# Two heads per 32-row strip, mixing folded into weights, last experts added by matmul: an edit of a two-layer hybrid kernel

## The chip, the cores and the metric

The kernel runs on one core of a Trainium2 chip. Its time is the device time of one launch in microseconds (us). The kernel before takes 791.38 us (median of three runs, 787.01 to 791.51).

## The reference

Input x is 4×256 rows of 256 f32 values. Eight residual stages follow each other, each fed by a layer norm without weights:

```python
x = x + attn_a0(norm(x))   # A: token mixing of neighbours, then a recurrence
x = x + ffn0(norm(x))      # F: the best of 8 experts, 256x256
x = x + attn_b0(norm(x))   # S: state space, with a convolution of 4 taps
x = x + ffn0(norm(x))      # G
x = x + attn_a1(norm(x))   # a: causal attention, 16 heads of 16, 4 key groups
x = x + ffn1(norm(x))      # e: the best 4 of 32 experts, width 96
x = x + attn_b1(norm(x))   # b: as a, with a slope per head times the distance
x = x + ffn1(norm(x))      # f
```

In stage A the change touches this part (xs is x shifted by one row; sequences are 256 rows):

```python
k = (x*tmk + xs*(1-tmk)) @ Wk.T + bk      # v likewise; r through silu
t = max(u + k, w)
e1, e2 = exp(-w - t), exp(u + k - t)
a = e1*a + e2*v ; b = e1*b + e2           # a recurrence over the rows
```

In stage S it touches conv = sum over 4 taps of shifted rows times conv_w, plus a bias, then silu, for 512 channels of h and 64 each of B and C. In f, y of an expert is (silu(x·gate)·(x·up))·down and is added with the weight of that expert among the row's four.

## The kernel before, in words

The 1024 rows are two groups g of 512, two sequences each, as four tiles of 128 rows. The residual x[g] stays on chip. Every stage of every group is a set of Python generators ("streams") named by stage letter, group and part: a0p is attention a, group 0, part p. follow() (L119) draws one step of a stream after another by the hand-written list ORDER. All engines work in order, so this one list is the program order of PE (TensorE), DVE (VectorE), ACT (ScalarE), POOL (GpSimd) and SP (which issues DMAs). BANKS is a second list: it says, tile by tile, which of the eight 2 KB PSUM banks is used. Nothing is reordered after it.

norm_steps (L221) makes mean and variance on DVE, the inverse root on POOL, the four normalised tiles xn on DVE (L239), then transposes them on PE and copies them as xnT on ACT.

Stage A, shift_mix (L265): mix(j) makes the mixed inputs for k, v, r (j = 0, 1, 2), each in two halves c: ACT scales the shifted rows (L293), DVE adds the own rows (L295). keys (L302) projects, makes low = min(k+u-w, 0) and top = max(k+u, w) on DVE (L308, L311), their exponentials on ACT, two scans and a reciprocal on DVE. values (L328) projects and scans, receive (L346) multiplies with r.

Stage S, state_space: conv (L588) has six channel tiles, four of 128 channels and B and C of 64 each; per tile a projection, an ACT scaling, three shifted multiply-adds on DVE (L602) and a silu.

Attention (L774), per group and layer: keys project all four key groups into kT, 32 rows each (16 dimensions, then rows that carry the key's number and causal flags), and keep it four times in kb, each copy with one key group unmasked (two copies by ACT L804, two by DVE). queries makes four projections pq, one head of each key group at a time (c), scaled into qT. Then four query units of 128 rows (sequence b, query tile qt; w = 128 or 256 keys). peaks (L842): scores pS as matmuls on 64 rows (L851; two strips r of the array side by side, masks in kb keep the two key groups apart), then for each head a DVE maximum (L864), which the profile shows as a maximum `junk` and a small read `nmx`. below (L870) transposes the maxima into the queries, qm. weights (L883): scores again, transposed, pST (L893, two strips at a time), ACT exponentials pT (L901), POOL's causal cut on the diagonal (L904). products (L909): pctx, four column strips of the array. finish divides, transposes, projects with Wo.

second_ffn (L984), stages e and f: route makes the four experts of a row and its place (128 places per expert). send scatters the rows by 16 indirect DMAs of POOL into `sent` in DRAM (L1046). For each of 16 pairs of experts: SP fetches xe (L1073), PE transposes, gate and up pgu, ACT silu, DVE product, PE transpose ph, DVE copy hT, PE py (L1118), DVE copy ye, SP writes `done` (L1124). back gathers by 16 indirect DMAs of POOL (L1134), add multiplies and adds on DVE (L1144), leave writes out.

Two matters decide the order around the change. First, SP's queue: in e and f the first fetch of group 1, which needs all 16 of its scatters, stands ahead of group 0's last done writes. Second, `sent` must have been cleared (stream cl, 512 KB writes) and the weights loaded (la, lf, ls, l1, lw) by SP at places in the same list.

Of the kernel before, what the change touches and what calls it, by code (L numbers as in the profile page):

```python
# [30 lines left out]
ROWS = E1 * CAP  # L31
NH, HP, NS = 8, 64, 64
# [3 lines left out]
UNITS = ((0, 0), (0, 1), (1, 1), (1, 0))  # L36


ORDER = """
k1 A0n kf x0*2 kf A1n A0n*2 x0 A0n x0 A0n*3 la A0n*4 lf x1 A1n x1 A0n ka A0m0 x1 A1n*2 A0n*2 A0m0  # L40
x1 A1n*2 A0m0 la lf A0m0 A0k0 A0m2*2 A1n*3 A0m1 A1n A0m1*3 A1n*2 A1m0 A0k0*4 A0k1*5 A0k0*2 ls A0k0
la A0v0 A1m0 la lf*2 A1n lf A1n A1m0*2 A0m2 A0b A0v0*2 A0k1 kf A0v0*2 A0k1 A0m2 ls A0k1 A0m2 ls*2
A1k0*3 A0v1 A0r0*2 A0v1*2 A1k0 A0v1 lf A0v1 A0r1*2 A1m1 A1k1 la A0o A1k1*4 A0o*4 F0r*2 A0o*3 F0r*2
A1m1*2 F0r A1m1 A1v1 lf*2 F0r A1k1*2 A1m2 F0r*3 A1v0 A1v1*3 F0r*3 A1k1 A1v1 k1*2 ks kf*3 F0r*5 ls
k1 A1k0*2 A1m2*4 F0r*3 F0s*4 A1v0*2 F0f A1v0 A1k0*2 A1v0 A1r0*2 A1r1*2 A1b A1o*3 F1r A1o ks*3
A1o*3 F1r*2 F0f F0t A1o F1r*2 PS F0t*2 F0f*2 F0t*2 F1r*4 F0e F1r*3 lf F0e*2 F0t F0e*2 F1r*5 F0e*2
F0r F0t F1r*4 F1s F0e*2 F1s F0t F0e*3 F1s*2 F0w F0b F0a S0n F0b*2 F1f F0a F0b F0a S0n*2 F0a S0n
F1f S0n F1t*3 F1w F1e F1t F1f*2 F1t ks*2 S0n*8 F1e*3 F1t*3 S0d*2 F1e*3 S0d*5 S0u*2 S0c*3 S0h S0u
S0c*2 F1e*2 S0h*2 S0g*2 S0h F1e*2 S0h*5 S0c*5 F1e S0h*4 F1b S0g*5 F1a S1n F1b*3 S0g k1 F1a S0c*2
F1a S1n*2 F1a S1n*2 cl*2 S0h*4 S0d*2 S1n*3 k1 S0l*2 S1n S0m*4 k1 S0l*3 S0h*3 k1 S0h cl S0h*2 S1n*4  # L50
S0l cl S0l*3 S1g*2 S1c S1d*2 S1c*4 S0u*2 S0h S0v*2 S0l*2 S0v S1d S0v*3 S0l S0v S0l S1d S0u*2 S1d
S0o S0u S1h S0v*5 S0y S1h S0o*2 S0y*2 S0l*2 S0y S0z S0o S1c S1h S1g S0z*2 S1h S0z S1d S1h S1c
S1h*4 S0l S0z S1c S0o*3 S1h S0z*4 S1c*2 S0z S1h S0z*3 S0y S0z*4 l1*2 G0r S1d S0l*4 S1u*2 S0l S1c
S1h*6 S1c S0z*2 S0l G0r S0l S1u*2 S1h*3 cl S0l S0y*2 S1h*3 S0y S0z*2 S1h l1 S0z S0o S0z S1g*2 S1d
cl S1v S1d S1v*7 S1m*4 S1l*2 S0z*5 S1l*2 cl S0z*4 S1v*2 S0z*2 S1u*2 S0z*2 G0r S1v*2 S1l*3 S0z*2
G0r*2 S1l*5 S1o S1y*2 G0r S1u G0r S1u G0r*2 S1y*2 S1z G0r*4 k1 S1o*3 S1z*3 G0r S1g*3 G0r*4 S1z
G0r*2 G0w G0s*4 S1z G0f S1z*3 S1l G0f S1z*2 S1l*10 S1z*5 S1l S1z S1y*3 S1z*2 S1o*3 G0t S1y G0f
G0t*2 G0f l1 S1z*2 G0e*3 G0t*2 S1z G0t G0e*2 G0t*2 G0e S1o S1z*2 G0e*2 G1r*2 S1z G0e*4 S1z*10 l1
S1z*3 G0b G1r G0b G1r*2 G0b*2 G1r*6 G0a k1*3 G1r*3 G0a a0n*2 G0a a0n G0a a0n*9 G1r*3 a0n a0k a0q
G1r P2 a0q cl a0a cl*2 a0q*5 G1r*2 G1w a0k*5 a0p k1 G0r k1 a0p k1 G1s a0p cl*2 a0q a0p*7 a0v l1*2  # L60
a0b G1r a0b cl*3 a0p*2 a0v a0p G1s*3 G1f G1t*2 G1f G1t*2 a0p*3 G1f G1t G1f a0p*3 G1e*6 G1t*2 a0b
G1e*2 a0p G1e G1t G1e*2 a0p*4 a0w*6 a0b a0p*5 a0w*4 a0c a0p G1e G1b*3 G1a*2 a1n a0w G1b a0w*6
a0b*2 a0c a0f*3 G1a a1n*2 a0w*3 cl G1a lw*3 a0w*9 a0c a1n a0w a1n*2 a0w*3 a0p a0w*4 a0f a1n*4
a0p*2 a0f a1a a0p a0f*2 a1n*3 a0f e0r a0p*2 a0c a1k a0w*4 a0b a0f a0b a1k a0f a1q*4 a0w*4 a0c
a0w*4 a1q a1k a0f a1k*3 a0w*3 a1p*2 a0f*2 a1q a0f e0r a0f*3 l1*2 a1q*2 a0f*2 a1p*4 a0c a0f*5 a1p*2
a0f*3 a1p a0f e0r*3 a1b*2 a1p e0r*4 a1w*5 a1p*3 e0r a1p*2 e0r*9 a1w a1v*2 a1w*2 a1p*2 a1w e0r*3
a1w a1c a1f a1p*2 a1b*2 e0s a1p*5 e0s*4 a1p a1w*7 a1p*4 e0s*2 a1p*3 a1w*2 a1c lw*2 e0s*3 a1w*3 e0s
a1p*2 a1w*4 lw*4 a1b*2 a1w*3 a1f*2 a1w a1f*2 a1p*2 a1c a1w*3 a1c a1f lw e0s*3 e0w a1f*2 e0s*2 a1b
lw*2 e1r lw a1f*2 a1w*5 a1f a1b a1w*10 a1c a1f*5 e0f*2 e0t e0f*2 a1w*2 a1f a1w e0t a1w a1c a1f e0t
a1f*5 e0t a1f e0g a1f*2 e0g*4 a1f e0t*4 e0h e0g a1f e1r*4 e0h*3 e0g*4 e0f*2 e0t e1r*4 e0g e0d*2  # L70
e1r*4 e0d*2 e1r e0h e0d*2 e0g e0t e1r*2 e0g e0h*3 e0t*2 e1r*2 e0g e1r e0f*3 e0d*2 e0g*4 e0t*2 e0f
e0t e0d*2 e0t*2 e1r*2 e1s*5 e0h*3 e0g*4 e0t*2 e0f e0d*4 e1s e0g*2 e0f e0g e0t*3 e0f e1s e0f e0h*4
e0d*2 e0g e0d e1s*2 e0g*4 e0d*3 e0t*2 e0h e0g e0t*3 e0h*3 e0d*2 e0f*2 e0h e0g*3 e0d*3 e0g e1s*2
e0g e0d*5 e0h e0g e0h*2 e0t*4 e0g*2 e0d*2 e0g e0d e0h*3 e0d*2 e1s*4 e0d e1s e1f*2 e0g*4 e0h*2 e0d
e0g e0d e0t e0g*2 e1f e0h e0d*2 e0g e0h e0d e0h*2 e0d*3 e1t*3 e1f e0d*2 e1t e1g*2 e0d*2 e0b e1t*2
e1g*2 e1t e1h e1g*3 e1f e1h*2 e1f e1g e1h e1d*2 e1f e0b*2 e1d*2 e1g e1t e1g*3 e1t*2 e0b e1t*3
e1h*3 e1d e1g e1h e1f*3 e0a*4 b0n e1g*4 e1t e1d*2 e1t*2 e1d*3 e0b*2 e0a e1d*2 e0a e1h*2 e0b e0a
e1g*5 e1t*3 e1h e1g e1h e1f*3 e1g e0b*3 e1t e1d*5 e1h e1w e1h e0a b0n e1h e1g*3 e1t*2 e1d*2 e1h
e1g e1d e0b e1h e0b*2 e1t e1g e1d e1f e0a e1d e0b e1g*2 e0a*2 e1f e1t*2 e0b*2 e1d*2 e1h e1d e0a*5
e1t e1g*3 b0n*2 e1h*4 e1g*3 b0n e1g*2 b0n*4 e1d*2 e1t*2 e1d*2 b0a e1h*3 e1g e1t b0n*3 e1d*4 e1g*2  # L80
e1t e1d b0n b0q*2 e1g*3 e1d e1h*2 b0k*3 e1d*3 b0q*2 e1h b0k*2 b0q b0k b0p*2 b0q*3 e1f e1t b0p*3
e1t e1g*2 b0p e1g e1d e1h e1d e1h e1d b0b*2 e1h*2 b0p*3 b0w*4 e1d*5 b0p b0w*2 e1d b0p*4 b0w b0p*2
b0w b0p*2 b0w*2 b0v*2 b0b*2 e1d e1b e1a e1b*3 b0p*2 b0w b0p*4 e1a*2 e1b*2 b0w*2 b0c b0p*2 e1a e1b
e1a b0f*3 e1b e1a e1b b0p*4 e1b b0w*6 e1a b0c b0w*3 b0f b0p*3 b0w*4 e1a b0f*3 b0c b0f b0b*2 b0p*2
b0f*2 e1a*2 b0w*6 b0f*2 b0w*2 e1b*3 b1n b0c e1b*3 b0p b0b b0w*3 b0b e1a*3 b0w e1a b0w*6 e1a b0w*4
b0c e1a b0w*4 b1n*4 b0f*5 b1n*2 b0c b0f*3 b1n*3 b0f*4 b1n*3 b1k f0r b1k*3 b0f b1k b0f b1q*2 b0f
f0r b0f b1k b1q e1r b1q*2 b1p f0r*7 b1q*3 f0r*2 b1p f0r*2 b1p*2 f0r b1p*2 b1b f0r*2 b1b b1w*2
f0r*3 b1p*2 b1w*2 b1a b1p b1w*2 f0r*2 b1v*2 b1p*4 b1w b1p b1w*3 b1c b1p*4 b1f*2 b1p b1f b1b*2
b1p*3 f0s b1f b1p*3 b1f f0s*5 b1w*7 f0s*4 b1c b1w*7 b1p*5 b1f b1p*2 b1b*2 b1f b1w*2 b1c b1f b1p*2
f0s*4 b1p*2 b1w*7 b1b b1f f1r b1c f0s*2 f0f b1w*6 f0f b1w b1f b1b b1w b1f b1w*2 b1c b1w*2 b1f*6  # L90
b1w*3 f1r f0t b1w*4 b1f*2 b1c f0t b1f*4 f0g b1f*2 f0t f0f b1f*3 f1r*3 f0t f0g*5 f0f*2 f0t*4 f0h*3
f0g f0t f0g f1r f0f f1r*7 f0f*2 f0d f0g f1r f0h f0d*3 f0t*2 f1r*2 f0h f0d f0g*2 f0h f1r f0g f1r*2
f0g*3 f0t*3 f0d*3 f0h f0g f0t*2 f1r*2 f1s f0h*3 f0g*6 f0f f0t f0d*2 f0h f0d f1w f1s f0h f0f*3
f1s*2 f0d*2 f0h*2 f0d f0t*4 f0g f1s*4 f0g*4 f0d*2 f0f f0d*3 f0t*2 f0d f1s f0h*4 f0g f0f*2 f0g f0t
f0g*3 f1s f0g f0h f1s f0d*3 f0g f0d f0h f0t*2 f0d*2 f0f f1s*2 f0g*2 f0d*2 f0t f0d f0h f0d f0h*3
f0g*3 f0d*2 f0t*4 f0d*2 f0g*2 f1s*3 f1f*2 f0h*2 f0d*2 f0g*2 f0r f1f f0d f0g f0h*2 f0t f0g f0d f0g
f0d f0h*2 f0d f0g f1t*2 f0g f0h f1t*2 f1f*2 f0d*3 f1g*5 f1h f1t*2 f0d*2 f1t*2 f0h f0d f1g*2 f1h
f0d f1g*3 f1t f1h f1f*2 f0d f1d f1g f1t*3 f1f f1g*2 f1h*2 f1t f1d f1f f1g*3 f1d*2 f0w f1t f1h*4
f0b f1f f1t*3 f1d*3 f1g*3 f1h f1f f1t f1d*2 f1g f0b f1d f0a f1h*2 f1t f1d*2 f0a f1d f1g*2 f1d*3
f0b*3 f0a f1h f1f*2 f0a f0b f0a f1h f0b*2 f1g*5 f0b*2 f1d*5 f1h f1t f1g*3 f1t*4 f1h f0a f1h*2 f0b  # L100
f1h f0a f1f f1d*3 f0a f1g*2 f1t*2 f1d f1g*3 f1h f1f f0a*2 f0b f1d*3 z0*2 f1g*2 f1d*2 f1h*2 f1g*2
f1t*2 f1h*2 f1f f0b*3 f1d*6 f1t*2 f1g*3 f1h*2 f1g*2 f1h*2 f1d f1t f1r f1t f1g f1d f0a f1d*3 f1h
f1d f1h f1g f0b f1g*2 f1d f1h*2 f1d*5 f1b f0a*5 f1a f1b f1a f1b*3 f1a f1b*2 f1a*4 f1b f1a f1b*2
f1a f1b f1a*2 f1b f1a z0*2 z1*3 f1b*3 f1a*3 f1b f1a z1
"""


# [22 lines left out]
def two_blocks(ctx: ExitStack, tc: tile.TileContext, a: dict, out: bass.AP):  # L130
# [134 lines left out]
    def shift_mix(n, g, fix):  # L265
# [98 lines left out]
        for j in range(3):  # L364
            streams[f"{n}m{j}"] = mix(j)
# [1263 lines left out]
```

## Time and profile before

| | us |
|---|---|
| median of three runs | 791.38 |
| the profiled execution | 788.77 |
| its span, first to last instruction | 787.0 |
| PE / DVE / ACT / POOL busy | 646 / 489 / 258 / 286 |
| mean granted TensorE clock | 0.908 |
| 0 to 77: loads, stage A | DVE 63.9 busy |
| 77 to 137: F; 137 to 251: S and G | PE 46.8; 101.1 |
| 251 to 392: attention a | PE 129.2, DVE 89.8 |
| 392 to 497: e | PE 87.4, DVE 55.9 |
| 497 to 645: attention b | PE 134.2, DVE 95.6 |
| 645 to 755: f | PE 97.5, DVE 57.8 |
| 755 to 787: last gathers and adds | POOL 16.0 |

The stages of both groups overlap, so the borders are rough. A group's line in the profile reads: line, engine, operation, out<-in, shape, count, then busy us, mean ns of one, then idle time of the engine before them and what ended it. PE records are hardware passes: a logical f32 matmul has two. Their ends are modelled, so the pace is read from the starts.

### The profile page before, as it was taken

Reading aid. Unit: us, or ns where it says so; the run is one execution under the profiler, and the core shown is the slowest. Engines: PE = TensorE matmul, PEld = TensorE weight load, DVE = VectorE, ACT = ScalarE, POOL = GpSimd, SP = SyncE. Lnnn points to the kernel's source line nnn. Section 1 sums busy time; section 2 is a strip of 40 time slices with the busy share of each in tenths; the row PEclk is TensorE's granted clock in tenths of the full one; section 3 lists DMA queues with packets and bytes.
Section 4 is the critical chain, followed back from the end, with each engine's and each line's share of the span. In section 5 each row is a group of like instructions: output and inputs, shape, how many; then the busy total and the mean of one; then the engine's idle time right before and its main releaser. Section 6 shows DMA issues by size and latency. Waiting matters only on the chain.

```text
span 787.0 us, 10048 instructions
## 1 busy us (share of the span) xinstructions
PE 645.9 (82%) x3168; PEld 433.4 (55%) x3168; DVE 488.6 (62%) x1507; ACT 258.3 (33%) x476; POOL 286.2 (36%) x333
## 2 busy tenths in 40 slices
PE   4667589999896999987994979999978999599930
PEld 2244454466584554443693978753444459498820
DVE  7987456898746677585371446577785637144642
ACT  4421135676431224322540222322520354122200
POOL 3114322434536224137216053136435431603435
PEclk9886989899996999998997898999997899899975
DMA  6602427000038237802245566212001124556833
GB/s 203 227 0 69 158 96 262 15 1 0 14 134 278 68 107 249 260 19 83 75 132 189 158 212 192 81 61 69 19 2 67 41 90 141 170 174 203 250 105 102
DMA packets 70827, 94.01 MB, mean 119 GB/s; under 512 B 6896, under 2 KB 60656, under 8 KB 70128
## 3 DMA queue, kind: packets, MB, share of 16 engines
q1 hardware_dynamic: 62944, 72.31, 28.3%
q0 software_dynamic: 7680, 20.98, 8.4%
q8 instruction: 27, 0.44, 0.3%
q14 instruction: 32, 0.26, 0.1%
q10 hardware_dynamic: 144, 0.01, 0.0%
HBM read 50.29 MB, written 42.99 MB: 119 GB/s over the span
## 4 chain that ended last, share of the span: by engine, by line
PE 53%; DVE 21%; issue 11%; POOL 5%; DMA 4%; another core or an unknown queue 4%; ACT 1%; POOLq 0%; DVEq 0%; ACTq 0%
PE pgu_f L198 9%; PE py_f L1118 6%; PE pST_b L893 3%; PE py_f L198 3%; PE px_f L1082 3%; PE pST_a L893 3%; PE pS_b L851 3%; DVE junk_a L864 2%; DVE cv L602 2%; PE pctx_b L915 2%; PE pS_a L851 2%; PE pq_b L198 2%; PE pq_a L198 2%; PE ph_f L1107 2%
## 5 line engine op out<-in xcount | busy, mean ns | idle before, releaser
L1134 POOL DMA_INDIRECT yb_f<-done,bk_f x64 | 65.0, 1016 | 110.7 <-issue 38.6
L198 PE MATMUL pgu_f<-gu,xT_f 128*128 128x192 f32 x512 | 97.4, 338 | 3.3 <-ACT xT_f L1086 3.3
L198 PEld LDWEIGHTS pgu_f<-gu,xT_f 128*128 128x128 f32 x512 | 88.4, 199 | 6.5 <-ACT xT_f L1086 4.6
L1046 POOL DMA_INDIRECT sent<-xn_f,to_f x64 | 62.8, 981 | 60.5 <-issue 19.5
L1118 PE MATMUL py_f<-dw,hT_f 96*128 96x256 f32 x256 | 67.6, 392 | 6.0 <-DVE hT_f L1110 5.5
L1122 DVE COPY ye_f<-py_f 128x512 f32<-128x512 f32 x64 | 43.8, 687 | 25.8 <-PE py_f L1118 8.9
L864 DVE CUSTOM_DVE_ANT_0 junk_b<-pS_b,tri 128x128 f32<-128x128 f32 (+1 forms) x128 | 45.8, 357 | 21.1 <-PE pS_b L851 14.2
L1098 ACT ACTIVATE he_f<-pgu_f 128x192 f32<-128x192 f32 x64 | 21.1, 332 | 106.4 <-PE pgu_f L198 53.6
L864 DVE CUSTOM_DVE_ANT_0 junk_a<-pS_a,tri 128x128 f32<-128x128 f32 (+1 forms) x128 | 45.7, 357 | 16.4 <-PE pS_a L851 6.6
L1118 PEld LDWEIGHTS py_f<-dw,hT_f 96*128 96x128 f32 x256 | 45.6, 194 | 13.2 <-ACT he_f L1098 4.4
L1086 ACT COPY xT_f<-px_f 128x512 f32<-128x512 f32 x64 | 36.6, 587 | 44.1 <-PE px_f L1082 22.6
L1100 DVE TENSOR_TENSOR he_f<-he_f,pgu_f 128x192 f32<-128x192 f32 x64 | 22.0, 349 | 46.4 <-ACT he_f L1098 33.8
L1110 DVE COPY hT_f<-ph_f 96x256 f32<-96x256 f32 x64 | 26.2, 415 | 29.2 <-PE ph_f L1107 19.0
L1144 DVE SCALAR_TENSOR_TENSOR x<-yb_f,wt_f,x 128x256 f32<-128x256 f32 x64 | 31.3, 495 | 19.7 <-DMA yb_f<-done,bk_f 19.2
L904 POOL TENSOR_SCALAR_AFFINE_SELECT pT_b<-pT_b 128x512 f32<-128x512 f32 x32 | 20.8, 669 | 57.2 <-ACT pT_b L901 57.0
L1107 PE MATMUL ph_f<-ident,he_f 128*96 128x128 f32 x128 | 24.5, 287 | 20.3 <-DVE he_f L1100 11.6
L901 ACT ACTIVATE pT_a<-pST_a 128x512 f32<-128x512 f32 x48 | 25.6, 604 | 41.0 <-PE pST_a L893 26.5
L901 ACT ACTIVATE pT_b<-pST_b 128x512 f32<-128x512 f32 x48 | 26.1, 599 | 39.0 <-PE pST_b L893 30.4
L904 POOL TENSOR_SCALAR_AFFINE_SELECT pT_a<-pT_a 128x512 f32<-128x512 f32 x32 | 20.0, 645 | 50.5 <-ACT pT_a L901 50.5
L1082 PE MATMUL px_f<-ident,xe_f 128*128 128x128 f32 x256 | 36.7, 275 | 0.0
L851 PE MATMUL pS_b<-kb_b,qT_b 64*128 64x256 f32 (+1 forms) x128 | 31.1, 561 | 3.1 <-DVE qm_b L878 3.1
L893 PE MATMUL pST_b<-qm_b,kb_b 64*128 64x512 f32 x96 | 31.4, 689 | 1.8 <-DVE qm_b L878 0.9
(298 smaller groups left out, 1341.7 us busy)
## 6 DMA issues: line engine op xcount, KB each, us to landing
xe_f<-sent SPq DMA_DIRECT2D x64, 256.0 KB
done<-ye_f SPq DMA_DIRECT2D x64, 256.0 KB
sent<-nil SPq DMA_DIRECT2D x16, 512.0 KB
xe_f<-fsent SPq DMA_DIRECT2D x16, 256.0 KB
fdone<-ye_f SPq DMA_DIRECT2D x16, 256.0 KB
gu<-in_L1f_gate SPq DMA_DIRECT2D x4, 768.0 KB
gu<-in_L1f_up SPq DMA_DIRECT2D x4, 768.0 KB
dw<-in_L1f_down SPq DMA_DIRECT2D x4, 768.0 KB
```

Source lines behind the costliest of these rows:

```text
L198: nc.tensor.matmul(dst, w(c), rhs(c), start=(c == 0), stop=(c == n - 1))
L851: nc.tensor.matmul(both[r][:, at:at + 2 * w].rearrange("p (s k) -> p s k", s=2), qT[rows, c, q0:q0 + P], kb[rows, 2 * r:2 * r + 2, b * S:b ...
L864: nc.vector.tensor_tensor_reduce(out=junk[:, :w], in0=both[r][:, at:at + w], in1=tri[:, S - w:], scale=1.0, scalar=NEG, op0=ALU.add, op1=A ...
L893: nc.tensor.matmul(pS, kb[rows, s, k0:k0 + P], qm[rows].rearrange("p c q -> p (c q)"), start=True, stop=True)
L901: nc.scalar.activation(pT.rearrange("p c q -> p (c q)"), pS, AF.Exp)
L904: nc.gpsimd.affine_select(pT, pT, pattern=[[0, AG], [1, P]], compare_op=ALU.is_ge, fill=zero, base=0, channel_multiplier=-1)
L1046: nc.gpsimd.indirect_dma_start(out=sent_to[g][t * TOPK + j], out_offset=bass.IndirectOffsetOnAxis(ap=to[:, t, j:j + 1], axis=0), in_=xn[:, ...
L1082: nc.tensor.transpose(px[:, j * P:(j + 1) * P], xe[q][:, k, c * P:(c + 1) * P], ident)
L1107: nc.tensor.transpose(ph[:, k * P:(k + 1) * P], h[q][:, k, :], ident)
L1118: nc.tensor.matmul(py[:, k * D:(k + 1) * D], hT[q][:, k, :], dw[:, 2 * q + k, :], start=True, stop=True)
L1122: nc.vector.tensor_copy(ye.rearrange("p k d -> p (k d)"), py)
L1134: nc.gpsimd.indirect_dma_start(out=yb, out_offset=None, in_=done[g], in_offset=bass.IndirectOffsetOnAxis(ap=kept_["back"][:, t, j:j + 1], ...
```

## The change

Six edits and a new list.

1. Layer norm: xn of tiles 0 and 2 is made by ACT (Identity with scale and bias), for which DVE makes `shift` = −mean·rstd.
2. Stage A: only r is mixed on rows. For k and v the mixing is in the weights: wk1 = wk·tm and wk·(1−tm), scaled once by ACT (streams kk, kv), and a projection has four matmuls, on xp and on xp shifted by one. low and top are each a Relu and an exponential on ACT.
3. Conv: B and C share one tile of 128 channels; the silu still writes them apart.
4. Attention: POOL packs two heads (16 columns each) into each 32-row strip of Wq and doubles Wk (stream pq; the wide Wq is loaded to a passing buffer). kT has two halves i, each with one head's rows unmasked and the added rows in the other's (BESIDE); kb is gone. Two projections pq in place of four. Scores pS and pST are matmuls on 32 rows, four strips in four banks at a time.
5. Last stage, group 1 only (END = 6): the scattered row also carries the row's number, experts and weights (INFO = 265 floats) into an own, cleared DRAM buffer (stream ce). The last six experts aren't written to DRAM: claim builds, per expert, a 128×512 matrix of weights on DVE, and collect adds their results by 24 matmuls in two banks and two DVE adds. Gathers of these experts read a zero row.
6. ORDER has 2395 steps in place of 2431 and is new from end to end, with loads and clears at other places; BANKS is new.

```diff
@@ norm_steps
+        nc.vector.scalar_tensor_tensor(shift, mv[:, :, 0], -1.0, rstd, ALU.mult, ALU.mult)
...
-            nc.vector.tensor_scalar(
-                xn[:, t, :], xg[:, t, :], mv[:, t, 0:1], rstd[:, t:t + 1],
-                ALU.subtract, ALU.mult)
+            if t % 2:
+                nc.vector.tensor_scalar(
+                    xn[:, t, :], xg[:, t, :], mv[:, t, 0:1], rstd[:, t:t + 1],
+                    ALU.subtract, ALU.mult)
+            else:
+                nc.scalar.activation(xn[:, t, :], xg[:, t, :], AF.Identity,
+                                     bias=shift[:, t:t + 1], scale=rstd[:, t:t + 1])
@@ shift_mix
+        def mixed(dst, w2, es):
+            xp = kept_["xp"]
+            dst = dst.rearrange("p (b s) -> p b s", b=2)
+            for i, t in enumerate(w2):
+                for c in range(NC):
+                    nc.tensor.matmul(dst, t[:, c, es], xp[:, c, :, 1 - i:S + 1 - i],
+                                     start=(i + c == 0), stop=(i + c == NC))
...
-            project(pk, lambda c: wk[:, c, es], lambda c: mixed[0][:, c, :])
+            mixed(pk, wk, es)
...
-            nc.vector.tensor_scalar(
-                flat(low), pk, bkuw[:, e:e + 1], 0.0, ALU.add, ALU.min)
-            nc.vector.tensor_scalar(
-                flat(top), pk, bku[:, e:e + 1], w[:, e:e + 1], ALU.add, ALU.max)
-            nc.scalar.activation(low, low, AF.Exp)
-            nc.scalar.activation(top, top, AF.Exp, bias=negw[:, e:e + 1], scale=-1.0)
+            nc.scalar.activation(flat(low), pk, AF.Relu, bias=minus[:, e:e + 1], scale=-1.0)
+            nc.scalar.activation(flat(top), pk, AF.Relu, bias=bkuw[:, e:e + 1])
+            nc.scalar.activation(low, low, AF.Exp, scale=-1.0)
+            nc.scalar.activation(top, top, AF.Exp, bias=neg2w[:, e:e + 1], scale=-1.0)
@@ first_block
+        def share(i, whole, part):
+            for t, by in ((part, tm), (whole, omt)):
+                for c in range(NC):
+                    nc.scalar.activation(t[:, c, :], whole[:, c, :], AF.Copy, scale=by[:, c, i:i + 1])
+                    yield
@@ state_space
-        tiles = [(DI + j * P, P) for j in range(4)] + [(2 * DI, NS), (2 * DI + NS, NS)]
...
-        streams[n + "c"] = conv((4, 5))
+        streams[n + "c"] = conv((4,))
@@ attention: keys, queries
-            kb = kept_["kb"] = pools["act"].tile([P, AG, TG], F32, tag="kb", name=f"kb_{name}", bufs=1)
...
+            for i in range(2):
+                nc.vector.scalar_tensor_tensor(
+                    kT[:, i, :].rearrange("p (b s) -> p b s", b=2),
+                    pk.rearrange("p (b s) -> p b s", b=2), half[:, i:i + 1],
+                    kaug[:, i, :].unsqueeze(1).to_broadcast([P, 2, S]), ALU.mult, ALU.add)
+                yield
...
-            for c in range(AH // AG):
+            for m in range(2):
...
@@ attention: peaks
-                    both = [bank("sq", f"pS_{n_}_{c0}_{r}") for r in range(2)]
+                    four = [bank("sq", f"pS_{n_}_{c0}_{s}") for s in range(AG)]
                     for c in range(c0, c0 + per):
-                        for r in range(2):
-                            rows, at = slice(64 * r, 64 * r + 64), (c - c0) * 2 * w
+                        for s in range(AG):
+                            rows, at = slice(32 * s, 32 * s + 32), (c - c0) * w
                             nc.tensor.matmul(
-                                both[r][:, at:at + 2 * w].rearrange("p (s k) -> p s k", s=2),
-                                qT[rows, c, q0:q0 + P],
-                                kb[rows, 2 * r:2 * r + 2, b * S:b * S + w],
-                                start=True, stop=True)
+                                four[s][:, at:at + w], qT[rows, c, q0:q0 + P],
+                                kT[rows, c % 2, b * S:b * S + w], start=True, stop=True)
@@ attention: weights
-                    for s0 in range(2):
...
-                        pairs = [(s, bank("st", f"pST_{n_}_{kt}_{s}")) for s in (s0, s0 + 2)]
-                        for s, pS in pairs:
-                            rows = slice(64 * (s // 2), 64 * (s // 2) + 64)
-                            nc.tensor.matmul(pS, kb[rows, s, k0:k0 + P],
-                                             qm[rows].rearrange("p c q -> p (c q)"),
-                                             start=True, stop=True)
+                    four = [bank("st", f"pST_{n_}_{kt}_{s}") for s in range(AG)]
+                    for s, pS in enumerate(four):
+                        rows = slice(32 * s, 32 * s + 32)
+                        for i in range(2):
+                            nc.tensor.matmul(
+                                pS.rearrange("p (c q) -> p c q", c=AG)[:, i::2, :],
+                                kT[rows, i, k0:k0 + P], qm[rows, i::2, :], start=True, stop=True)
+                    yield
@@ second_ffn
+                if end and q == 2:
+                    nc.sync.dma_start(
+                        info, sent_[through * 2 * CAP:, D:].rearrange("(k p) d -> p k d", k=end))
...
-                nc.sync.dma_start(rows(done[g], q), ye)
+                due["ye", q] = ye
+                if q < through:
+                    nc.sync.dma_start(rows(done_, q), ye)
...
+        def claim():
...
+            for i in range(end):
...
+                nc.vector.tensor_scalar(
+                    to, numbers, info[:, i, 0:1], sw[:, i, :], ALU.is_equal, ALU.mult)
+        def collect():
+            two = [bank(k, f"pend_{name}_{k}") for k in ("acc", "st")]
+            for i in range(end):
+                q, k = through + i // 2, i % 2
+                for t in range(NT):
+                    nc.tensor.matmul(
+                        two[t // 2][:, t % 2 * D:(t % 2 + 1) * D],
+                        due["to", i][:, t * P:(t + 1) * P], due["ye", q][:, k, :],
+                        start=(i == 0 and t % 2 == 0), stop=(i == end - 1 and t % 2 == 1))
+                yield
+            for t in range(0, NT, 2):
+                xt = x[g][:, t:t + 2, :]
+                nc.vector.tensor_tensor(
+                    xt, two[t // 2].rearrange("p (k d) -> p k d", k=2), xt, ALU.add)
+                yield
@@ load_1, pack
+                for m in range(2):
...
+                    nc.gpsimd.tensor_copy(to[:, :, :, i * AD:(i + 1) * AD], by[:, :, :, :AD])
```

## The prediction

> **What bounds the kernel now.** First the page's busy shares and its chain of waits, then the same engines stage by stage, then the groups of the stages that the change touches, then two stretches of the PE timeline.
>
> ```profile
> PE 53%; DVE 21%; issue 11%; POOL 5%; DMA 4%; another core or an unknown queue 4%; ACT 1%; POOLq 0%; DVEq 0%; ACTq 0%
> PE pgu_f L198 9%; PE py_f L1118 6%; PE pST_b L893 3%; PE py_f L198 3%; PE px_f L1082 3%; PE pST_a L893 3%; PE pS_b L851 3%; DVE junk_a L864 2%; DVE cv L602 2%; PE pctx_b L915 2%; PE pS_a L851 2%; PE pq_b L198 2%; PE pq_a L198 2%; PE ph_f L1107 2%
> ```
>
> TensorE carries half of the chain, VectorE a fifth, and no single line more than 9%: many stages, each with its own limit. So I cut the span at the stage borders. Columns: window, length, then busy us of PE, weight loads, DVE, ACT, POOL, then granted clock, DMA share, GB/s.
>
> ```profile
> 0.00:77.00 77.00, 49.75 (x127) 26.82 (x128) 63.87 (x123) 24.09 (x33) 22.21 (x36) 0.82 0.38 127
> 137.00:251.00 114.00, 101.05 (x475) 69.13 (x473) 82.90 (x175) 57.21 (x96) 50.61 (x61) 0.92 0.23 78
> 251.00:392.00 141.00, 129.18 (x631) 68.86 (x632) 89.78 (x395) 47.86 (x93) 53.42 (x68) 0.96 0.37 121
> 497.00:645.00 148.00, 134.24 (x619) 68.10 (x618) 95.60 (x386) 49.06 (x92) 59.14 (x68) 0.93 0.17 53
> 645.00:755.00 110.00, 97.51 (x590) 88.72 (x588) 57.76 (x157) 30.84 (x68) 33.14 (x33) 0.95 0.57 179
> 755.00:787.00 32.00, 0.00 (x0) 0.00 (x0) 10.48 (x22) 0.00 (x0) 16.00 (x16) 0.55 0.37 109
> ```
>
> 0–77 (token mixing) is DVE's: 63.9 of 77 us busy. The two attention windows (251–392, 497–645) are PE's, busy 91–92%, with DVE at 64% behind it. The last 32 us are 16 gathers.
>
> ```profile
> L893 PE MATMUL pST_b<-qm_b,kb_b 64*128 64x512 f32 x96 | 31.4, 689 | 1.8 <-DVE qm_b L878 0.9 <-ACT pT_b L901 0.4 <-issue 0.4
> L851 PE MATMUL pS_b<-kb_b,qT_b 64*128 64x512 f32 x64 | 21.7, 720 | 3.1 <-DVE qm_b L878 3.1
> L198 PE MATMUL pq_b<-xnT_b,wqb 128*128 128x512 f32 x32 | 14.9, 599 | 0.0
> L864 DVE CUSTOM_DVE_ANT_0 junk_b<-pS_b,tri 128x256 f32<-128x256 f32 x64 | 27.1, 424 | 11.4 <-PE pS_b L851 7.2
> L864 DVE DVE_READ_ACCUMULATOR2_ANT nmx<- 128x1 f32 x256 | 21.2, 83 | 0.2
> L295 DVE SCALAR_TENSOR_TENSOR mix<-xp,vec,mixtmp 128x512 f32<-128x512 f32 x12 | 9.4, 812 | 0.0
> L308 DVE TENSOR_SCALAR low<-pk,bkuw 128x512 f32<-128x512 f32 x4 | 2.9, 719 | 0.0
> L311 DVE TENSOR_SCALAR top<-pk,bku,vec 128x512 f32<-128x512 f32 x4 | 3.2, 801 | 0.0
> ```
>
> Operands here have 64 rows, half the array, and each logical f32 matmul is two hardware passes (96 records for 48 matmuls). The means contain the modelled end of a pass; the pace is read from starts: 512 columns 0.430 us a pass (286.483 to 286.912 in one strip), 256 columns 0.216.
>
> **The change, part by part** (all of it summed against the span of 787.0).
>
> *Token mixing, 0–77.* DVE loses 8 of 12 mix (8×0.812=6.5), low and top (4×0.719+4×0.801=6.1), half of the normalised tiles (4×0.54+4×0.44=3.9): 16.5, less small new ones about 0.5: 16 of 63.9. ACT loses 8 mixtmp of 0.72 and gains 8 Relu of about the same, 8 weight scalings at about 0.37 (half a 512-wide row) and 8 normalised tiles of about 0.5: 24 → about 31, still low. PE gains 16 logical matmuls, 32×0.43=13.8 us, at 33 us streamed in the window → 47. Key and value projections no longer wait for mix on DVE, but now wait for the scaled weights (wk, wv loads, then ACT), which lie under the x loads and norms. Bounds: all 16 if DVE sets the whole window, nothing if PE's 13.8 fill the hole, or +3 if ACT stands in front. DVE's busy share is 0.83, but the first 20 us are load; I take −9.
>
> *Conv, in 137–251.* Per group three DVE operations (0.74), two 512-column matmuls (4×0.43=1.7) and one ACT go: DVE −4.4, PE −3.4. Conv is in the chain (cv L602, 2%). I take −4; zero if state_space is held by PE (101 of 114).
>
> *Normalised tiles to ACT*, all other stages: 2×0.48 us of DVE per norm and group leave; ACT's work runs parallel with the odd tiles. The chain holds about 12 us of these rows, so a third, −4; the new `shift` operation (under 0.1 us, 83 ns is the row of a tiny one) costs about 1 back. Net −3.
>
> *Attention.* Per group and layer PE streams pq 16×0.43=6.9 → 3.4; pS 10.4 → 5.2; pST 48×0.43/2=10.3 → 5.2; the rest (pv, pm, pctx, pu, pcT, po, pt, pk, about 17) stays. That is 13.8 × 4 = 55 us less PE work. DVE stays: 64 row maxima per group and layer remain (424+83 and 291+83 ns), 28.2 of about 41.5; two mask products (2×0.48) go and one extra key add (about 0.7) comes, so 40.5. The chain inside these two windows holds pST 46.9, pS 34.4, pq 28.1: halved, −54.7 is the ceiling. But DVE has 90 of 141 and 96 of 148, a floor about 50 us below each window's length, and every score step now has to clear four banks: 8 maxima × 0.5=4 us (0.9 us of PE makes them), or four exponentials of 0.6=2.4 us.
>
> Does a four-strip step really take a quarter? Row first: in the 64-row case the two strips start
>
> ```profile
> 286.48 1.88 PE L893 MATMUL pST_a<-qm_a,kb_a 64*128 64x512 f32 x8
> 286.49 0.19 PEld L893 LDWEIGHTS pST_a<-qm_a,kb_a 64*128 64x128 f32 x2 [0.24 <-issue]
> 295.01 1.06 PE L915 MATMUL pctx_a<-pT_a,vaug 128*32 128x512 f32 x8
> ```
>
> 8 passes of 512 in 1.88 (starts 7 ns apart, loads too), and pctx, four column strips, 8 passes in 1.06 us. At 264.88 strip A starts its next pass before the other strip's earlier-issued one. Strips thus run on their own. The Trainium skill ("TensorE: Matmul & The Clock Gate", section "Part 3: Packing small matmuls — row/col tiling") says the contrary for this point: matmuls start and end in strict program order. New pST gives strip 0 its two matmuls (four passes of 256), then strip 1, and so on. By the rule a step would take about (16−3)×0.216=2.81 us against 1.72, 24 steps: +26 us on PE; by the row 0.86, −20.6 (both for all four group-layers together). No four-row-strip run is in this trace; I take the row. Against the gain also speaks "TensorEngine Tiling (Array Packing)", section "PSUM Bottleneck": after packing, copying out of PSUM may become the limit. The row agrees here: 16 maxima×0.507=8.1 us per late query unit against 3.4 → 1.7 of PE. So I take half the ceiling, −27; bounds 0 and −54.7 (+26 if strict order).
>
> Packing of Wq: about 20 small POOL copies, no row of its kind; between 0.2 (smallest POOL op) and 1.05 us (bias add): 4–9 us, these are small too, so I take the low end, on POOL, which is at 51 of 114. Hidden; bare, up to 9. The 4.3 MB more of clearing sit on DMA at share 0.23 there; bare they'd be some 25 us at 170 GB/s, but nothing needs them before the last sends, 400 us later. SP has nine more issues, none of which waits.
>
> *Last experts.* The list ends with the same 16 gathers at one per 1.30 us (20.8). They need the last done write; that is now pair 12, not 15. Between these, PE does py 13–15 and ph 14–15, 3.05 us: −3. Claim (6 masks, about 0.7=4.2 us DVE) and collect (48×0.216=10.4 us PE) lie under the gathers; bare they'd cost 10.4+1.4.
>
> ```profile
> 753.62 1.13 PE L1118 MATMUL py_f<-dw,hT_f 96*128 96x256 f32 x4 [0.51 <-DVE hT_f L1110]
> 759.74 1.00 POOL L1134 DMA_INDIRECT yb_f<-done,bk_f  x1 [18.37 <-DMA out<-x]
> 761.04 1.00 POOL L1134 DMA_INDIRECT yb_f<-done,bk_f  x1 [0.30 <-issue]
> ```
>
> The info read stands on SP behind a fetch that waits for the same sends: no new wait. The stalls of SP's done writes behind group 1's first fetch (about 16 us in each routed stage) stand in the new list as before: the fetch has five done writes behind it now as then. Rest of the list: −1.
>
> Sum: −9 −4 −3 −27 −3 −1 = −47 → span 740, with 1.8 outside 741.8 as the profiled execution's time. That one (788.77) stood 2.6 below the median 791.38; taking half of this spread back would give 743, and I keep 742.
>
> **Rivals.**
> 1. *DVE holds attention.* PE's saving only widens its idle time: DVE maxima and exponentials on ACT set each unit, attention −3 instead of −27 → about 766. For: DVE's share of the chain is 21%, and the 256-wide maxima of layer b wait only 7.2 us for pS in all. Against: DVE is only 64% busy in these windows.
> 2. *All follows PE*: attention −54.7, mixing −13 → about 710. For: PE 92% busy. Against: the four-bank steps.
> 3. *Slower.* Four PSUM banks are needed at once per score step, and all engines are in order: PE stands at the step until the last of the four is cleared, with projections of the next stage behind it, who feed DVE. 8 maxima are 4 us, four exponentials 2.4. There are 24 pST steps and 24 pS steps; the other gains (20) plus the PE saving (27) are used up from about 1.0 us per step, 48×1.0; at 1.4 us it ends at 807. For: before, two banks were needed at once. Against: eight banks, handed out by the list, which reuses the longest freed ones.
> 4. *Doesn't do what it says*: strict order on the array and mixing shifted to PE, gains cancel: about 785–790.
>
> **How the numbers follow.** Main case 0.51 at 742 (own range 728–755); DVE holds 0.23 at 766; all PE 0.15 at 710; slower 0.06 at 807; nothing 0.05 at 787. Range 708 to 773 leaves out the last two and the tails of the others. About 1% is what a measurement of this kernel can tell from no change: faster 0.89, same 0.05, slower 0.06.
>
> **What would show it.** Right: in the attention windows PE's streamed work is down by about 27 us each and a pST step's 16 passes take 0.9–1.1 us from first to last start; the maxima stay at 424 and 83 ns with less idle "<-PE pS"; the mixing window's DVE is near 48 us; 16 gathers at 1.30 us still end the kernel, collect under them. Wrong: a pST step near 2.8 us (strict order), PE idle released by ACT pT or DVE nmx grown by tens of us (banks), ACT becoming the releaser of mixing, or the gathers starting later than 4 us after pair 12's write.

## The result and the profile after

The changed kernel takes 782.87 us (median of 15 runs, 778.69 to 789.9) beside 788.66 for the kernel before: ratio 0.9933, interval 0.9904 to 0.9961. It is faster by 0.7%, where 742, 6%, was forecast, with a range of 708 to 773. The profiled execution has a span of 777.9 (787.0 before). All runs came in series, each on one chip, and the series are of two kinds, without which no number below can be read: in some the kernel before takes 788 to 791, as here, in others 738.6 to 739.1; in those the change gives 2.9%. Every ratio is taken against the kernel before in the same series.

The chain of waits of the changed kernel, by engine and by line, and its busy times by stage (columns as before):

```profile
PE 49%; DVE 20%; issue 8%; another core or an unknown queue 6%; ACT 6%; DMA 6%; POOL 4%; POOLq 0%; SPq 0%; DVEq 0%; ACTq 0%
PE pgu_f L207 9%; PE py_f L1167 6%; PE px_f L1131 3%; DVE junk_a L888 3%; PE py_f L207 3%; DVE junk_b L888 2%; PE pST_a L917 2%; PE pST_b L917 2%; PE pctx_b L939 2%; PE ph_f L1156 2%; DMA yb_f<-fdone,bk_f 2%; PE pS_b L878 1%; DVE x L1231 1%; PE pctx_a L939 1%
```

```profile
0.00:72.00 72.00, 55.10 (x161) 29.83 (x162) 51.94 (x113) 29.27 (x47) 21.33 (x33) 0.93 0.52 171
248.00:387.00 139.00, 117.77 (x816) 73.49 (x815) 81.88 (x362) 46.23 (x88) 52.30 (x83) 0.84 0.49 155
493.00:640.00 147.00, 117.67 (x817) 73.89 (x816) 93.38 (x378) 48.70 (x91) 56.89 (x67) 0.83 0.16 51
640.00:778.00 138.00, 107.15 (x634) 97.62 (x632) 71.91 (x191) 30.14 (x68) 50.58 (x49) 0.90 0.53 160
```

Stage borders, set at the same events in both traces (the last Wo product of a stage, the first key projection of the next), give the account: mixing 77 → 72, F to G 176 → 176, attention a 139 → 139, e 111 → 106, attention b 142 → 147, f 142 → 138. The two attention stages of the kernel before, by these borders:

```profile
253.00:392.00 139.00, 127.61 (x626) 67.61 (x626) 87.85 (x389) 47.68 (x93) 52.75 (x68) 0.96 0.38 122
503.00:645.00 142.00, 128.24 (x588) 63.33 (x587) 93.66 (x381) 46.35 (x87) 57.23 (x67) 0.93 0.16 49
```

So of the attention stages, where 27 of the 47 us were to come from, one gave nothing and the other lost 5. Their groups of instructions did change as planned:

```profile
L917 PE MATMUL pST_b<-qm_b,kT_b 32*128 32x256 f32 x192 | 25.7, 512 | 5.2 <-issue 2.1 <-DVE qm_b L902 1.2 <-ACT pT_b L925 1.1
L207 PE MATMUL pq_b<-xnT_b,wqb 128*128 128x512 f32 x16 | 7.4, 597 | 0.0
L888 DVE CUSTOM_DVE_ANT_0 junk_b<-pS_b,tri 128x256 f32<-128x256 f32 x64 | 27.1, 423 | 15.9 <-remote 12.0 <-PE pS_b L878 0.7
L335 ACT ACTIVATE low<-pk,minus 128x512 f32<-128x512 f32 x4 | 2.7, 683 | 7.7 <-PE pk L324 7.7
```

pq has half its passes, the maxima cost the same 423 ns, low is on ACT. What is new stands behind junk_b: 12.0 us of idle time ended by "remote", a releaser that the trace can't name (behind junk_a it grew from 3.1 to 12.2). The same shows in the chain as "another core or an unknown queue", up from 4% to 6%: in attention a and b from 7.9 us to 24.0. Its pieces in the changed kernel (start, length):

```profile
279.64 4.74 another core or an unknown queue
...
348.11 7.37 another core or an unknown queue
...
525.67 4.35 another core or an unknown queue
...
598.09 7.55 another core or an unknown queue
```

The second of them, over all engines (start, length, engine; in brackets the idle time before and its releaser):

```profile
348.69 2.08 PE L917 MATMUL pST_a<-qm_a,kT_a 32*128 32x256 f32 x8
348.79 0.98 POOL L1091 DMA_INDIRECT sent<-xn_f,to_f  x1 [0.30 <-issue]
...
352.63 0.98 POOL L1091 DMA_INDIRECT sent<-xn_f,to_f  x1 [0.30 <-issue]
355.46 0.29 DVE L888 CUSTOM_DVE_ANT_0 junk_a<-pS_a,tri 128x128 f32<-128x128 f32 x1 [7.41 <-remote]
...
355.68 1.09 ACT L925 ACTIVATE pT_a<-pST_a 128x512 f32<-128x512 f32 x2 [22.36 <-remote]
```

PE started the last pS passes that this maximum reads before 347.4, and pST by 350.2. Yet the increments of PE's semaphore (the counter by which an engine tells the others that its work is done) stop at 344.47, and the six that are due come all together from 355.43 to 355.72; DVE and ACT, which wait for them, start at 355.46 and 355.68. Meanwhile POOL is sending out eleven scatters, from 339.73 to the last at 352.63. I call this a hold. Over the whole trace PE's increments come over 1 us behind the modelled end of their matmul by 48 us in sum before (longest 4.4) and 87 after (longest 10.5), each time while POOL's scatters or gathers run. These sums are upper figures: the records of about 30 of nearly 800 increments are missing from each trace; with every increment set only against the last matmul that ended before it, they are 18 and 33. PE stands idle from 351 to 357. Its granted clock is at half from 331 to 365, but not because of this hold alone: it fell before it, and falls at this place (324 to 351) in a trace without holds too.

### The profile page after: what moved, and what is told of

It is laid out like the page before. It is cut to its first block, busy times and chain, and to the rows that moved or that the text cites. A ratio compares the mean times of both kernels' runs of the same rounds, so it can differ in the third digit from the quotient of the medians.

```text
span 777.9 us, 11040 instructions
## 1 busy us (share of the span) xinstructions
PE 634.0 (81%) x3656; PEld 459.4 (59%) x3656; DVE 465.9 (60%) x1488; ACT 266.3 (34%) x503; POOL 292.1 (38%) x357
## 4 chain that ended last, share of the span: by engine, by line
PE 49%; DVE 20%; issue 8%; another core or an unknown queue 6%; ACT 6%; DMA 6%; POOL 4%; POOLq 0%; SPq 0%; DVEq 0%; ACTq 0%
PE pgu_f L207 9%; PE py_f L1167 6%; PE px_f L1131 3%; DVE junk_a L888 3%; PE py_f L207 3%; DVE junk_b L888 2%; PE pST_a L917 2%; PE pST_b L917 2%; PE pctx_b L939 2%; PE ph_f L1156 2%; DMA yb_f<-fdone,bk_f 2%; PE pS_b L878 1%; DVE x L1231 1%; PE pctx_a L939 1%
## 5 line engine op out<-in xcount | busy, mean ns | idle before, releaser
L207 PE MATMUL pgu_f<-gu,xT_f 128*128 128x192 f32 x512 | 93.5, 330 | 2.7 <-ACT xT_f L1135 2.6
L207 PEld LDWEIGHTS pgu_f<-gu,xT_f 128*128 128x128 f32 x512 | 84.4, 192 | 4.9 <-ACT xT_f L1135 3.4
L1221 POOL DMA_INDIRECT yb_f<-done,bk_f x48 | 49.6, 1034 | 94.9 <-DVE x L1231 27.8
L1167 PE MATMUL py_f<-dw,hT_f 96*128 96x256 f32 x256 | 69.8, 398 | 16.0 <-ACT he_f L1147 11.1
L1091 POOL DMA_INDIRECT sent<-xn_f,to_f x48 | 47.1, 982 | 46.0 <-ACT xT_f L1135 16.2
L888 DVE CUSTOM_DVE_ANT_0 junk_a<-pS_a,tri 128x128 f32<-128x128 f32 (+1 forms) x128 | 45.7, 357 | 25.1 <-remote 12.2
L917 PE MATMUL pST_a<-qm_a,kT_a 32*128 32x256 f32 x192 | 25.8, 458 | 10.9 <-DVE nmx L888 8.6
L1131 PEld LDWEIGHTS px_f<-ident,xe_f 128*128 128x128 f32 x256 | 31.2, 144 | 5.3 <-issue 3.1
L202 POOL TENSOR_TENSOR rstd_f<-var_f,neghalf 128x4 f32<-128x4 f32 x8 | 8.2, 1026 | 64.9 <-DVE var_f L241 64.9
```

The source lines that it names most:

```text
L207: nc.tensor.matmul(dst, w(c), rhs(c), start=(c == 0), stop=(c == n - 1))
L888: nc.vector.tensor_tensor_reduce(out=junk[:, :w], in0=four[s][:, at:at + w], in1=tri[:, S - w:], scale=1.0, scalar=NEG, op0=ALU.add, op1=A ...
L917: nc.tensor.matmul(pS.rearrange("p (c q) -> p c q", c=AG)[:, i::2, :], kT[rows, i, k0:k0 + P], qm[rows, i::2, :], start=True, stop=True)
L1091: nc.gpsimd.indirect_dma_start(out=sent_to_[t * TOPK + j], out_offset=bass.IndirectOffsetOnAxis(ap=to[:, t, j:j + 1], axis=0), in_=xn[:, t ...
L1131: nc.tensor.transpose(px[:, j * P:(j + 1) * P], xe[q][:, k, c * P:(c + 1) * P], ident)
L1167: nc.tensor.matmul(py[:, k * D:(k + 1) * D], hT[q][:, k, :], dw[:, 2 * q + k, :], start=True, stop=True)
```

## The experiments

Three theories went into them. H: the holds took the gain. C: PE, less busy, is granted half its clock more often (0.96 → 0.84 and 0.93 → 0.83 in the attention windows) and gives the saved passes back. D: VectorE's maxima set attention, the first rival of the prediction.

**Scatters left out.** Group 0's scatters of e and f, which lie inside attention, are not issued; in both kernels.

```diff
+                    if g:
                         nc.gpsimd.indirect_dma_start(
```

> The changed kernel without the 32 scatters of group 0 in stages e and f (the ones that lie inside the two attention stages); rows then come as zeros, so this leaves out part of the computation. Theory H (PE's semaphore increments come late while POOL runs indirect DMAs back to back, and the changed kernel stands in such holds for 24 us of its attention chain against 8 before): 15 to 22 us less than the changed kernel, 761 to 768. Theory D (VectorE's maxima set attention): at most 5 less, 778 or more. Theory C (PE, less loaded, is granted half its clock and gives the saved passes back): at most 8 less, since idle time for the clock remains.

> The kernel before without the same 32 scatters (the same part left out). Theory H: 4 to 9 us less than before, about 782, clearly less gain than in the changed kernel. D and C: the same gain as in the changed kernel to within 3 us, whatever it is.

Measured: 717.42 against 738.7 for the kernel before (0.970, 0.963 to 0.977); the kernel before with the same edit 740.75 (1.002, 0.999 to 1.005). The number that matters was one that no theory had: the kernel before, unaltered, took 739, 50 us less than in the first series. The unaltered change wasn't beside them, so they told nothing between the theories yet.

**More passes, badly placed.** Each score matmul issued twice in a row.

```diff
+                            for _ in range(2):
                                 nc.tensor.matmul(
```

> The changed kernel with each score matmul (pS and pST) issued twice to the same place: 41 us more of PE passes by 0.86 us a step, so PE has in scores what it had before. Theory C: the clock in attention returns from 0.84 to about 0.93 and the time stays within 5 us of the changed kernel. D: within 5 us too, with the clock no matter. H: 5 to 15 more. If PE's passes set attention after all: 25 to 40 more, 808 to 823.

Measured 816.25 (1.091, 1.084 to 1.099). The number lies among those expected, but against another start: the unaltered change takes 0.971 in a series of this kind (below), so this edit costs some 89 us, where at most 40 were expected. The trace says why: the edit cost far more than 0.86 us a step. One pST step of this kernel, then one of the unaltered change in such a series, both at full granted clock:

```profile
266.62 4.69 PE L919 MATMUL pST_a<-qm_a,kT_a 32*128 32x256 f32 x31
```

```profile
288.63 1.17 PE L917 MATMUL pST_a<-qm_a,kT_a 32*128 32x256 f32 x16
```

From first to last start the 16 passes take 0.79 us, the 32 take 4.53 (the last of them lies outside the window of this view). In the unaltered change each strip has four passes in a row, here eight, and here the next strip starts only when the one before is at its fifth. Most of the 24 steps in this trace are like it. So this run doesn't weigh PE's load; a_ps2 does.

**Half of the maxima.**

```diff
-                        for c in range(c0, c0 + per):
+                        for c in range(c0, c0 + per if s % 2 else c0):
...
-                        nc.scalar.activation(pT.rearrange("p c q -> p (c q)"), pS, AF.Exp)
+                        nc.scalar.activation(pT.rearrange("p c q -> p (c q)"), pS, AF.Exp, scale=1e-6)
```

> The changed kernel with half of the maxima (strips 1 and 3 alone) and exponentials of scores scaled to near zero so that they stay finite; this leaves out part of the computation. VectorE has 56 us less in attention (half of 4 x 28.2). Theory D: 25 to 45 us less, 738 to 758. H: 5 to 12 less, since the holds stay. C: 0 to 10 less.

Measured 697.36 (0.945, 0.940 to 0.949), in the series where the kernel before takes 739; its reading needs the unaltered change in such a series.

**The two kernels unaltered.** The edit of each: none.

> The changed kernel, unaltered, beside the kernel before on the chip of this call. In the last call the kernel before took 738.7 where it had taken 788.7, and no late semaphore increment stood in the four traces. Theory H (holds ate the gain): where the kernel before takes about 739 the change gives 25 to 40 us, 700 to 714; where it takes about 788 again, 6 us as before. Theories C and D (clock, VectorE): about 0.7% in either case, 733 or 783.

> The kernel before, unaltered, for its trace on the chip of this call. Theory H: where it takes about 739, PE's increments are never more than 1 us behind the modelled end of their matmul (48 us of such lateness in the first trace), and the chain has no piece without a known releaser over 2 us. C and D: the difference of 50 us lies elsewhere, and such lateness stays.

Here the kernel before took 790.76 and the changed one 786.03 (0.9935, 0.9897 to 0.9972); b_again agreed with before (0.998, 0.994 to 1.002). Lateness of PE's increments, summed as above: 49 us in b_again, 75 in a_again. So the first result and its holds come back in a second series. What makes a series of one kind or the other is not known: the record numbers the chips, and number 9 stands for a series with 791.11 for the kernel before and, four minutes later, for one with 738.78. In the series of a_again b_halfmax gave 783.53 (0.9905, 0.987 to 0.994), 7 us, as expected where PE leads:

> The kernel before with half of the maxima (one of each pair) and exponentials of scores scaled to near zero; this leaves out part of the computation. VectorE loses 56 us in attention. If PE bounds attention there, 5 to 15 us less than before; if VectorE bounds it as much as in the changed kernel, 20 or more less.

**The change and both edits in a series of the other kind.**

> The changed kernel, unaltered. The kernel before has taken 788 to 791 twice and 738.7 once, where the four traces show no late increment. Theory H: where the kernel before takes about 739 beside it, the changed one takes 700 to 725, 2 to 5% less; where it takes about 790, 0.6% less as twice before. C and D: 0.7% less in both cases.

> The changed kernel without group 0's 32 scatters in e and f (part of the computation left out), on the same chip as the unaltered one. Theory H: where the kernel before takes about 790, 12 to 25 us less than the changed kernel beside it; where it takes about 739, within 8 us of it, since POOL's scatters alone (1.3 us each) lie beside other work. C and D: within 8 us in both.

> The kernel before without the same scatters. Theory H: where before takes about 790, 5 to 12 us less than before, less than the changed kernel gains by it; where it takes about 739, no change (it was 0.2% there). C and D: the same gain in both kernels.

Measured, beside 738.57: the changed kernel 719.75 (0.971, 0.963 to 0.980), without scatters 718.66 (0.970), the kernel before without scatters 740.02 (1.003). C and D had 0.7% for the change here and are out by that; H had 2 to 5% (in a_again's expectation still 25 to 40 us, which was too much). In this series the scatters cost nothing, as all three theories allowed, and the change gives 19 us. The same moment as above, in the trace of a_third, with scatters at the same pace:

```profile
341.27 1.11 PE L952 MATMUL pu_a<-ident,cu_a 128*128 128x128 f32 x4
...
341.82 0.29 DVE L888 CUSTOM_DVE_ANT_0 junk_a<-pS_a,tri 128x128 f32<-128x128 f32 x1
...
342.32 1.66 PE L917 MATMUL pST_a<-qm_a,kT_a 32*128 32x256 f32 x7
342.41 0.97 POOL L1091 DMA_INDIRECT sent<-xn_f,to_f  x1 [0.30 <-issue]
```

The maximum that stood for 7.4 us starts without a wait. In none of the traces from series of this kind is an increment of PE late by 1 us.

**Maxima, passes and POOL's pace**, beside 739.05:

> The changed kernel with half of the maxima and near-zero exponents (part of the computation left out), now beside the kernel before with the same. D: at least 15 us more gained by it than by the kernel before (which gained 7 where it took 791; this one gained 22 against the unaltered changed kernel, over two chips). C and PE-bound: both gain the same to within 6 us.

> The kernel before with half of the maxima (the same left out). D: 3 to 10 us less than before, since PE sets its attention stages. C and PE-bound: as much as the changed kernel gains, 20 us.

> The changed kernel with every set of pS passes run twice (the whole set again, so that the strips stay side by side): 24 steps of 0.86 us, 21 us more of PE in attention, and PE less idle. C: granted clock up by 0.03 or more and at most 5 us more time, or less time. D: 5 us more at most, clock no matter. PE-bound: 15 to 25 us more.

> The changed kernel with a POOL operation of 1.0 us after each of group 0's scatters and gathers in e and f, so that they go out every 2.3 us in place of 1.3. If a hold lasts as long as POOL's run of indirect DMAs goes on: where the kernel before takes about 790, either holds break up (10 us or more gained against the changed kernel, 1.5% or more under before) or, if a hold ends with the last scatter whatever the pace, 5 to 20 us more. Where it takes about 739: 0 to 5 us more than the changed kernel's 0.971 of before, as POOL lies beside.

```diff
-                    for c in range(c0, c0 + per):
+                    for c in (*range(c0, c0 + per), *range(c0, c0 + per)):
...
+                    if g == 0:
+                        nc.gpsimd.tensor_tensor(gap, half4, neghalf, ALU.pow)
```

Half of the maxima: the changed kernel 695.71 (0.942, 0.935 to 0.949), from 0.971, so 22 us; the kernel before 729.65 (0.989, 0.981 to 0.997), 8 us. The difference of 14 is just under the 15 that D had. D is right in part: of 56 us less DVE work the changed kernel turns 39% into time, the old one 14%. a_ps2: 732.83 (0.992, 0.989 to 0.995), 15 us more for passes worked out at 20.7 us (24 × 0.86). That is neither C nor D, but the low end of what was expected if PE's passes set attention: the clock did rise (granted in attention a from 0.89 to 0.95), and the time with it. Attention stages of the unaltered change (a_third), then of a_ps2:

```profile
249.00:373.00 124.00, 111.92 (x816) 71.33 (x815) 81.43 (x363) 46.35 (x89) 51.63 (x82) 0.89 0.54 174
...
461.00:589.00 128.00, 111.86 (x815) 70.10 (x814) 92.54 (x378) 47.99 (x89) 57.07 (x67) 0.88 0.18 58
```

```profile
249.00:377.00 128.00, 114.31 (x1058) 76.77 (x1057) 81.38 (x362) 44.48 (x86) 51.69 (x82) 0.95 0.54 166
461.00:595.00 134.00, 118.61 (x1059) 79.25 (x1058) 94.80 (x385) 45.74 (x87) 59.26 (x67) 0.91 0.19 60
```

In the unaltered change PE is 87 to 90% busy, DVE 66 to 72%. Less DVE work shortens the time and more PE work lengthens it, neither at its full price: the reading that fits is that a step of PE and its maxima follow one another in one chain, and that neither engine's total is the bound.

a_spaced: 758.74 (1.027, 1.020 to 1.035), 41 us more than the change, where 0 to 5 were expected. 64 operations of about 1.07 us (68 us) did not lie beside other work: the causal cuts of pT queue behind them on POOL (PE's idle time before pctx that ended with such a cut is 12.5 us in its trace, and none in that of the unaltered change). That group 0's x also comes later from its gathers is likely but was not measured, so most of the 41 us stays unassigned. What it was made for, the length of a hold, it couldn't tell, as its series has none.

**Scatters left out where there are holds, and single edits undone.**

> The changed kernel without group 0's 32 scatters in e and f (part of the computation left out). H: where the kernel before takes about 790, a ratio of 0.965 to 0.98 against the unaltered change's 0.9934 there, 12 to 25 us less; where it takes about 739, 0.97 as twice before. If the holds seen in the traces cost nothing: 0.99 to 1.0 where before takes about 790.

> The changed kernel with edit 5 undone: all 32 experts of the last stage written to memory and gathered, no masks and no adding matmuls, the list otherwise kept. By the prediction 3 us more than the changed kernel (ratio 0.975 where before takes 739, 0.997 where it takes 790). If the end is set by the sends' stall and by the gathers' pace alone: no difference, 0.971 or 0.993.

Beside 791.11: a_nosend3 767.93 (0.973, 0.966 to 0.980), against 0.9934 for the change there: 16 us back (11 to 22 by the interval of a_nosend3 alone), as H had it. The trace shows where: of the four pieces "another core or an unknown queue" in attention only the first is left, 4.66 us at 279.92 under four of POOL's gathers; the three under scatters are gone. The attention stages of a_nosend3:

```profile
249.00:379.00 130.00, 114.21 (x817) 72.52 (x816) 82.07 (x363) 46.17 (x89) 37.04 (x67) 0.89 0.49 150
484.00:622.00 138.00, 118.77 (x817) 74.28 (x816) 93.23 (x378) 48.66 (x91) 41.13 (x51) 0.83 0.13 39
```

Each is 9 us shorter than in the changed kernel with its scatters (139 and 147), the second at the same granted clock of 0.83, so that a lower clock is not what took those 9. Both are still 6 and 10 us longer than in series without holds (124 and 128, above).

a_end0 793.79 (1.004, 1.000 to 1.008): undoing the matmul ending costs 8 us. Its list was made for the ending, so the first of group 1's gathers is issued ahead of the last pairs' writes (part of the computation may be left out) and waits with the rest; 8 is what the edit is worth in this list, not by itself.

> The kernel before without group 0's 32 scatters in e and f (part of the computation left out). H: where before takes about 790, 4 to 10 us less (0.987 to 0.995), about half of the 16 to 18 that the changed kernel gained by it; where it takes about 739, no change (1.002 and 1.003 so far). If the holds ate the same from both kernels: 16 or more where it takes about 790.

> The changed kernel with all four normalised tiles on VectorE again (edit 1 undone, the small shift operation kept). By the prediction 3 us more and some 2 of the mixing stage, 4 to 6 in all: ratio 0.977 to 0.979 where before takes 739, 0.999 where it takes 790. If these tiles lie beside other work: no difference, 0.971 or 0.993.

Beside 738.78: b_nosend3 740.97 (1.002, 0.999 to 1.005), in a series without holds again, so that the kernel before without scatters was not measured where there are holds. a_xn 722.37 (0.977, 0.971 to 0.983) against 0.971: 4 us, as forecast, though the intervals overlap, so that it can't be told from none.

## Why the prediction was wrong

**The step that failed, twice over, is attention's −27.**

First, in series of the forecast's kind, by 13 us of the total: the change gives 6 us there and 19 without holds. The cost that the sum put at nothing is the wait of DVE and ACT for PE's late increments. Leaving out group 0's scatters gives 16 us back there and nothing elsewhere, and the pieces under these scatters go from the chain. That this takes more from the changed kernel than from the kernel before is read from the stages: with holds the two attention stages of the kernel before are 6 and 10 us longer than without (138.4 and 142.2 against 132.4 and 132.1), those of the changed kernel 15 and 19 (138.9 and 147.1 against 124.1 and 128.3), 17 us more in all; outside attention the same pairs of traces differ less in the changed kernel, 27 us against 34. The prediction copied "another core or an unknown queue 4%" into its first fence, 29 us of the chain, and gave it no term. It took the one stall that it did see, in e and f under group 1's scatters, for SP's queue: stage e of the kernel before takes 111 us there and 90 in a series without holds, and 19.5 us of its chain there are such pieces. No rival had a wait of this kind. Whether what holds the increments back is on PE's side, POOL's or the DMA engines' stays open, as does why only some series have it; that the changed kernel waits longer in a hold (10.5 us against 4.4) is seen, and its cause is not shown.

Second, where there are no holds the two attention stages gain 8.3 and 3.8, 12 in place of 27. The stages of the kernel before, from the trace of b_nosend2 (those of the changed kernel stand above, from a_third):

```profile
254.00:386.00 132.00, 124.08 (x622) 66.08 (x622) 86.70 (x389) 46.88 (x91) 36.03 (x52) 0.99 0.36 112
476.00:608.00 132.00, 125.16 (x589) 61.24 (x588) 94.31 (x381) 45.76 (x87) 40.99 (x51) 0.94 0.12 37
```

"Half the ceiling" was the term, with PE and DVE taken as two loads and the larger as the floor. In the first series the chain's PE entries for scores and queries did fall by 47 us, near the ceiling of 54.7, and in their place came 16 us of unnamed pieces, 22 of DVE (9 of them maxima), 8 of ACT and 8 of issue. a_halfmax2 and a_ps2 show the prices: 0.39 us per us of maxima, 0.74 per us of passes, so that both weigh. That is rival 1 by half. The four banks of rival 3 may weigh too: 24 pST steps take 34 us from first to last start in a_third, where 0.79 each would be 19; half clock and waits for banks share the difference, unseparated.

The measured 783 is nearest to the fourth rival, 785 to 790, and only by number: its reason, strict order on the array, did not come about.

**The other terms**, stage by stage in series without holds (19.0 in all; the trace of b_nosend2 stands for the kernel before, which it equals within 0.3%):

- Mixing −9: 4.6. DVE fell by 12 (63.9 → 51.9 busy), not 16, and ACT, absent from the chain before, holds 12 us of it after (in the first series' trace): the bound "if ACT stands in front" came in part.
- Conv and norms −7: group 1 leaves G 12.5 us earlier, so they work, but group 0's first key projection is only 4.8 earlier, hardly more than after mixing: on the way to attention next to nothing; the rest of the lead can show only in a's second half. Edit 1 by itself is worth 4 by a_xn.
- The tail −3: from the last stage's scatters to the end 89.2 → 85.9, 3.3, as worked out; but stage f as a whole takes 128 us in both, so its way to the scatters grew by as much. Undone in its own list the edit is worth 8 where there are holds.
- e gave 2.1, where −1 stood for the rest of the list.
- Packing of Wq and clearing hidden: right (the wqa and wqb copies are 3.0 us of POOL in all; the last of wqa starts at 218 in a_third, its first use at 245).

**The four-strip step** was right: 0.79 us from first to last start, where 3 × 0.216 = 0.65 stands behind the 0.86 that was worked out and 12 × 0.216 = 2.59 behind the 2.81 of strict order. The rule that I set against the row, matmuls in strict program order (the Trainium skill, "TensorE: Matmul & The Clock Gate", "Part 3: Packing small matmuls — row/col tiling"), doesn't hold for starts across strips here; but a_double shows that this has a limit, between four and eight passes in a row, which the row of two strips didn't show.

The Trainium skill's warning in "TensorEngine Tiling (Array Packing)", "PSUM Bottleneck", that reading out of PSUM may become the limit after packing, agrees in part: half of the maxima, which read PSUM, weigh 22 us after packing in place of 8, but they don't set the time alone.

## What to carry to other kernels

Give every entry of the chain a term, above all those without a name: the 29 us of "unknown" were over three times the 9 that the span gained. Where two engines hand work to each other step by step, price each per us by a run that takes a little from it (half of the maxima, one more set of passes) before counting the saving of one against the total of the other. And time a change in more than one series, with the kernel before beside it each time, before explaining it.

## What the hardware showed that was not expected

- The same kernel takes 791 us in some series and 739 in others, with runs that spread by 1.0 to 1.5% within one. In the first kind PE's semaphore increments arrive up to 10.5 us late while POOL's indirect DMAs run, in the second never by 1 us.
- Four row strips of 32 run side by side with four passes of 256 columns in a row on each (16 passes in 0.79 us), but not with eight (32 passes in 4.53 us).
- In the longest hold (418 to 429, stage e) PE's granted clock falls to half from 419 to 433; in the series without holds the clock of this stage is 1.00. Passes at half clock go at half pace: pST passes of 256 columns start every 0.43 us at 349, 0.216 in the steps at full clock.
